# Two attentions on one core: image loads moved behind the copies of f and g, those copies on two queues, and the last reciprocals taken from PSUM

## Chip, cores, metric

The kernel runs on one core of one Trainium2 chip. The metric is the device time of one execution in microseconds (us). Ratios are the mean time of one kernel's runs over that of the other's from the same rounds, so they are not quite the ratio of the medians that I quote beside them.

## The reference, cut to what matters

```python
# x: (8, 64, 64, 64) float32, n = 4096 positions an image
f, g, hh = Wf@x + bf, Wg@x + bg, Wh@x + bh        # 8, 8 and 64 channels
beta = softmax(f^T g, axis=2)                      # 4096 x 4096 an image
x = x + hh @ beta^T                                # layer 0
xn = group_norm(x); q, k, v = split(w_qkv @ xn + b)
x = x + w_proj @ (softmax(q^T k / 8) v)^T + b_proj  # layer 1
```

## The kernel before

An image is two halves of 2048 columns on 64 partitions each. Every layer of every image is four chunks of 512 columns per half; a chunk is 16 steps of scores (TensorE), exponentials (ScalarE), weighted sums (TensorE) and running sums of the exponentials (VectorE). The parts that the change touches:

```python
    def load_x(b):                                  # four loads of 256 KB by SyncE
        ...
                nc.sync.dma_start(t[ts(h, C), ts(k, NH // 2)], x[b, ...])
    load_x(0)                                       # at the very start
    ...
        def project(self, k):                       # f and g of half the columns
            ...
            nc.scalar.activation(full, ps, AF.Identity, bias=fgb)
            nc.vector.tensor_copy(high, full)
            nc.vector.scalar_tensor_tensor(split, high.bitcast(F32), lowmask, full, ...)
            for j in range(2):
                for h in range(2):
                    for p in range(2):
                        for i, (dst, half) in enumerate(((self.f, h), (self.g, p))):
                            nc.sync.dma_start(dst[rows, cols], split[ts(2*j+i, 32), half, :])
    ...
        # finish(): the sums of a chunk, three works for later steps
            def sums(spare):                        # TensorE, ScalarE copy, four small DMAs
            def reciprocals():                      # 128x8, to DRAM, broadcast back to r
            def result():                           # raw * r, then residual and output
    ...
    for b in (1, 2):
        load_x(b)                                   # scheduled early: SyncE is free then
    ...
    # after all chunks: check that every reciprocal lies in range, count the bad ones
    reg = nc.values_load(n_bad[0:1, 0:1], ...)
    with tc.If(reg > 0):
        general_path(tc, *args)                     # a slow path for sums out of range
```

Instructions are placed on each engine's stream by a scheduler at build time, by readiness and then by program order.

## Time and profile before

| | us |
|---|---|
| median of six runs | 3189.54 (3187.82 to 3190.85) |
| span in the trace | 3188.0 |
| first exponential | 22.49 |
| fourth, tenth exponential | 25.22, 35.04 |
| half-clock stretch of TensorE at the start | 20.44 to 30.68 |
| last weighted sum ends | 3169.25 |
| result of the last chunk | 3181.91 |

The page and the timeline are shown in the prediction. In all views SPq, ACTq and PEldq are the sequencers of SyncE, ScalarE and TensorE, which issue copies, wait and branch. Here are lines of the chain of waits at the start (start, length, what), then two groups by source line (durations min/median/max in ns, first and last start):

```profile
16.85 1.50 SPq L381
19.03 2.54 DMA fg_l<-split_l
22.49 2.86 ACT e_l L623 x3
26.20 4.97 PE acc_l L122 x12
```

```profile
L312 DVE RECIPROCAL stash<-zh_l x64: 193/203/205, 98.7 to 3175.1; 128x8 f32<-128x8 f32 x64
L64 PEldq COMPARE_BRANCH  x1: 3595/3595/3595, 3178.6 to 3178.6; - x1
```

The reader sees a start that goes from SyncE's issues to the landing of a copy, to exponentials, to twelve weighted sums at half clock (4.97 us; later dozens take 2.73 in the same chain). The branch on the flag takes TensorE's sequencer 3.6 us (3178.56 to 3182.16), hidden before because the last chunk still waits for its transfer (landed at 3180.34, result at 3181.91). The 128x8 operations of 203 ns in the prediction are the reciprocals of L312.

### The profile page before, as it was taken

The page shows a single profiled execution, that of the slowest core. Times are in us where ns is not written, and L with a number is a line of the kernel's source. Part 1 is how long each engine was busy: PE and PEld are TensorE (multiplying, and loading weights), DVE is VectorE, ACT ScalarE, POOL GpSimd, SP SyncE. Part 2 cuts the span into 40 slices and gives each one's busy share as a digit, 9 for nine tenths or more (in the row PEclk, how much of TensorE's full clock was granted, in tenths as well). Part 3 has the DMA queues.
Part 4 walks back from the last instruction along what each step waited for, and adds up shares of the span by engine and source line. Part 5 has one row for each costly group of instructions (what it writes and reads, how often), then busy time and mean ns, then how long its engine had stood idle before and what let it go on. Part 6 is the DMA issues. An engine that isn't in the chain of part 4 may idle for free.

```text
span 3188.0 us, 58576 instructions
## 1 busy us (share of the span) xinstructions
PE 3116.8 (98%) x25525; PEld 1106.0 (35%) x25525; DVE 2450.2 (77%) x1588; ACT 2083.4 (65%) x2257; POOL 16.7 (1%) x41
## 2 busy tenths in 40 slices
PE   7999999999999999999999999999999999999997
PEld 2333334333333334333333333333333333334432
DVE  6899766887678876788767887679866798666665
ACT  6787655776557765577655875558855587555554
POOL 2000000000000000000000000000000000000000
PEclk9999999999999999999999999999999999999999
DMA  3100010100101001010010100101001000000000
GB/s 69 34 8 17 11 34 8 28 21 8 35 8 28 21 8 34 8 28 21 8 34 8 31 19 7 38 5 35 18 5 41 2 21 18 5 21 15 9 14 15
DMA packets 66408, 63.54 MB, mean 20 GB/s; under 512 B 39408, under 2 KB 39488, under 8 KB 66144
## 3 DMA queue, kind: packets, MB, share of 16 engines
q1 hardware_dynamic: 65024, 59.56, 7.9%
q8 instruction: 202, 3.31, 0.4%
q14 instruction: 62, 0.51, 0.1%
q0 software_dynamic: 800, 0.15, 0.0%
q10 hardware_dynamic: 320, 0.01, 0.0%
HBM read 25.33 MB, written 8.65 MB: 11 GB/s over the span
## 4 chain that ended last, share of the span: by engine, by line
PE 87%; ACT 5%; DVE 4%; issue 2%; DMA 1%; SPq 0%; DVEq 0%; ACTq 0%
PE acc_l L122 51%; PE s_l L122 31%; ACT e_l L623 5%; DVE esum_l L595 3%; PE z_l L122 2%; PE qk_l L122 1%; PE v_l L122 1%; DMA r_l<-recips 0%; PE fg_l L122 0%; SPq L306 0%; DMA zt_l<-zs_l 0%; DVE split_l L371 0%; DVE vt_l L276 0%; DMA recips<-stash 0%; DMA x<-in_x_dram 0%
## 5 line engine op out<-in xcount | busy, mean ns | idle before, releaser
L623 ACT ACTIVATE e_l<-s_l 128x1024 f32<-128x1024 f32 x2048 | 1967.5, 1025 | 1062.0 <-PE s_l L122 1062.0
L595 DVE TENSOR_TENSOR esum_l<-esum_l,e_l 128x2048 f32<-128x2048 f32 x896 | 2050.6, 2289 | 390.1 <-ACT e_l L623 347.3
L122 PE MATMUL acc_l<-e_l,vt_l 64*64 64x512 f32 (+1 forms) x12288 | 1959.5, 595 | 6.7 <-DVE raw_l L524 5.9
L122 PE MATMUL s_l<-kq_l 64*64 64x512 f32 x8192 | 992.2, 589 | 1.5 <-DVE ve_l L443 1.5
L122 PEld LDWEIGHTS acc_l<-e_l,vt_l 64*64 64x64 f32 (+1 forms) x12288 | 594.2, 134 | 1067.2 <-issue 963.9
L122 PEld LDWEIGHTS s_l<-kq_l 64*64 64x64 f32 x8192 | 343.7, 133 | 543.0 <-issue 534.7
L122 PE MATMUL s_l<-fg_l 32*128 32x512 f32 x2048 | 272.0, 472 | 23.6 <-ACT e_l L623 15.5
L122 PEld LDWEIGHTS s_l<-fg_l 32*128 32x128 f32 x2048 | 108.0, 182 | 345.0 <-ACT e_l L623 213.2
L595 DVE TENSOR_TENSOR esum_l<-e_l,e_l 128x2048 f32<-128x2048 f32 x64 | 146.2, 2285 | 78.4 <-ACT e_l L623 78.4
L320 DVE TENSOR_TENSOR raw_l<-raw_l,r_l 128x512 f32<-128x512 f32 x64 | 44.0, 688 | 84.7 <-DMA r_l<-recips 84.7
L310 DVE TENSOR_TENSOR zh_l<-zt_l 128x8 f32<-128x8 f32 x64 | 10.5, 164 | 106.4 <-DMA zt_l<-zs_l 106.4
L122 PE MATMUL z_l<-esum_l,ones 128*32 128x512 f32 x512 | 68.4, 606 | 1.5 <-DVE vt_l L276 1.3
L524 DVE COPY raw_l<-acc_l 128x512 f32<-128x512 f32 x32 | 22.1, 690 | 41.5 <-PE acc_l L122 41.5
L302 ACT COPY zs_l<-z_l 128x512 f32<-128x512 f32 x64 | 38.2, 597 | 5.1 <-PE z_l L122 5.1
L498 ACT ACTIVATE kq_l<-qk_l,qkb 128x512 f32<-128x512 f32 x64 | 40.7, 697 | 0.0
L122 PE MATMUL qk_l<-xn_l,wqk 64*64 64x512 f32 x256 | 34.8, 611 | 0.0
L122 PE MATMUL v_l<-wvp,xn_l 64*64 64x64 f32 x1024 | 22.1, 223 | 8.4 <-ACT e_l L623 8.4
L122 PEld LDWEIGHTS v_l<-wh,x 64*64 64x64 f32 x1024 | 23.0, 136 | 15.9 <-issue 13.6
L122 PE MATMUL fg_l<-x,wfg 64*64 64x512 f32 x128 | 18.8, 652 | 9.7 <-DVE low L164 9.7
L122 PEld LDWEIGHTS v_l<-wvp,xn_l 64*64 64x64 f32 x1024 | 18.4, 134 | 18.6 <-ACT e_l L623 14.9
L525 DVE TENSOR_TENSOR raw_l<-acc_l,raw_l 128x512 f32<-128x512 f32 x32 | 22.1, 692 | 3.3
L528 DVE SCALAR_TENSOR_TENSOR raw_l<-raw_l,pb,x 128x512 f32<-128x512 f32 x32 | 24.0, 751 | 0.9
(81 smaller groups left out, 299.1 us busy)
## 6 DMA issues: line engine op xcount, KB each, us to landing
fg_l<-split_l SPq DMA_DIRECT2D x256, 64.0 KB, 2.0
r_l<-recips SPq DMA_DIRECT2D x128, 128.0 KB, 2.9
x<-in_x_dram SPq DMA_DIRECT2D x32, 256.0 KB, 4.8
kq_l<-kq_l SPq DMA_DIRECT2D x64, 128.0 KB, 2.3
out_dram<-raw_l SPq DMA_DIRECT2D x64, 128.0 KB, 2.3
zt_l<-zs_l SPq DMA_DIRECT2D x256, 2.0 KB, 1.8
recips<-stash SPq DMA_DIRECT2D x64, 4.0 KB, 1.4
wqk<-in_WqkvT_dram POOLq DMA_DIRECT2D x2, 32.0 KB, 5.3
```

Of the source, the lines that this page charges most:

```text
L122: in_order(nc.tensor.matmul(*args, **kwargs))
L302: nc.scalar.copy(zs, z)
L310: nc.vector.tensor_add(zh, zt[:, 0, :], zt[:, 1, :])
L320: nc.vector.tensor_mul(raw, raw, r)
L498: nc.scalar.activation(self.parts[:, h, cols], ps[:, h, :], AF.Identity, bias=k1["qkb"][:, h : h + 1],)
L524: nc.vector.tensor_copy(raw, acc[0])
L525: nc.vector.tensor_add(raw, acc[1], raw)
L528: nc.vector.scalar_tensor_tensor(o, o, k1["pb"], x_tiles[self.b][:, ts(c, CW)], op0=ALU.add, op1=ALU.add)
L595: nc.vector.tensor_add(esum, first if t == 1 else esum, e)
L623: nc.scalar.activation(e[:, p], ps, AF.Exp, scale=at.scale)
```

## The change

The intent: take loads that nobody needs yet out of the way of the start; issue 16 small copies from two engines; and end without three transfers in series.

```diff
+            queues = (nc.sync, nc.scalar) if self.b == 0 else (nc.sync, nc.sync)
...
-                            nc.sync.dma_start(
+                            sent = queues[i].dma_start(
...
-    for b in (1, 2):
-        load_x(b)
+    with tc.issue_after(layers0[0].sent.ins):
+        for b in (1, 2):
+            load_x(b)
...
+            def at_once():                          # the last chunk only
+                z = ps_s.tile([P, 2, CW], F32, tag="s", name=f"z_{n}")[:, 0, :]
+                for p in range(2):
+                    for h in range(2):
+                        matmul(z[ts(h, C), :], ones, esum[:, p, h, :], start=p == 0, stop=p == 1)
+                nc.vector.reciprocal(r, z)
+                result()
+                bounds(r, 1)
...
+    bounds(stash, 0)                                # the other 504 columns, apart
     while later:
         later.pop(0)[2]()
...
+    matmul(bad_ps, bad[:, 0:1], ones[:, 0:1], start=True, stop=False)
+    matmul(bad_ps, bad[:, 1:2], ones[:, 0:1], start=False, stop=True)
```

(`ones` becomes 64 wide, the stash loses eight columns, and `bounds` holds the four operations of the old check.)

More of the change, by code (lines that the diff above doesn't have):

```diff
@@ L62 @@
     fast_path(tc, n_bad, *args)
-    reg = nc.values_load(n_bad[0:1, 0:1], min_val=0, max_val=P)
+    reg = nc.values_load(n_bad[0:1, 0:1], min_val=0, max_val=2 * P)
     with tc.If(reg > 0):
@@ L177, in fast_path @@
     make_identity(nc, ident)
-    ones = const.tile([P, 32], F32, name="ones")
+    ones = const.tile([P, C], F32, name="ones")
     nc.vector.memset(ones, 1.0)
@@ L197, in fast_path @@
     QP = 2 * CW // P
-    stash = const.tile([P, 2 * B * NC * QP], F32, name="stash")
+    stash = const.tile([P, (2 * B * NC - 1) * QP], F32, name="stash")
     recips = [dram.tile([P, QP], F32, name=f"recips_{i}") for i in range(2 * B * NC)]
@@ L297, in sums @@
                         matmul(
-                            z[ts(2 * h + p, 32), :], ones, esum[:, p, h, :],
+                            z[ts(2 * h + p, 32), :], ones[:, 0:32], esum[:, p, h, :],
                             start=True, stop=True, tile_position=(0, 32 * (2 * h + p)),
@@ L317, in reciprocals @@
                     nc.sync.dma_start(r[ts(h, C), :], row.partition_broadcast(C))
+            def at_once():
+                z = ps_s.tile([P, 2, CW], F32, tag="s", name=f"z_{n}")[:, 0, :]
+                for p in range(2):
+                    for h in range(2):
+                        matmul(
+                            z[ts(h, C), :], ones, esum[:, p, h, :], start=p == 0, stop=p == 1
+                        )
+                nc.vector.reciprocal(r, z)
+                result()
+                bounds(r, 1)
             def result():
@@ L321, in result @@
                 self.residual(raw, c)
+            if index == 2 * B * NC - 1:
+                return (at_once,)
             return sums, reciprocals, result
@@ L384, in project @@
                             )
+                            if i == 0:
+                                self.sent = sent
         def scores(self, ps, t, p, c):
@@ L601, in weigh @@
                 delay = NT
-            sums, reciprocals, result = at.finish(acc, esum, c, i)
+            works = at.finish(acc, esum, c, i)
+            if len(works) == 1:
+                at_step(now, works[0])
+                return
+            sums, reciprocals, result = works
             at_step(now + delay, lambda: sums(spare), not spare)
@@ L633, in fast_path, with bounds @@
         weigh(*r, len(seq) * NT)
+    bad = const.tile([P, 2], F32, name="bad")
+    bad_ps = ps_a.tile([P, CW], F32, tag="a", name="bad_ps")[0:1, 0:1]
+    def bounds(recip, i):
+        ok = work.tile(list(recip.shape), F32, tag="zs", name=f"ok_{i}")
+        nc.vector.tensor_scalar(ok, recip, 1.0 / SUM_MAX, None, op0=ALU.is_ge)
+        nc.vector.scalar_tensor_tensor(
+            ok, recip, 1.0 / SUM_MIN, ok, op0=ALU.is_le, op1=ALU.mult
+        )
+        least = small.tile([P, 1], F32, tag="least", name=f"least_{i}")
+        nc.vector.tensor_reduce(least, ok, axis=AX.X, op=ALU.min)
+        nc.vector.tensor_scalar(bad[:, i : i + 1], least, -1.0, 1.0, op0=ALU.mult, op1=ALU.add)
+    bounds(stash, 0)
     while later:
         later.pop(0)[2]()
-    ok = work.tile(list(stash.shape), F32, tag="zs", name="ok")
-    nc.vector.tensor_scalar(ok, stash, 1.0 / SUM_MAX, None, op0=ALU.is_ge)
-    nc.vector.scalar_tensor_tensor(ok, stash, 1.0 / SUM_MIN, ok, op0=ALU.is_le, op1=ALU.mult)
-    least = small.tile([P, 1], F32, tag="least", name="least")
-    nc.vector.tensor_reduce(least, ok, axis=AX.X, op=ALU.min)
-    bad = small.tile([P, 1], F32, tag="bad", name="bad")
-    nc.vector.tensor_scalar(bad, least, -1.0, 1.0, op0=ALU.mult, op1=ALU.add)
-    ps = ps_s.tile([P, 2, CW], F32, tag="s", name="bad_ps")
-    matmul(ps[0:1, 0, 0:1], bad, ones[:, 0:1], start=True, stop=True)
-    nc.vector.tensor_copy(n_bad, ps[0:1, 0, 0:1])
+    matmul(bad_ps, bad[:, 0:1], ones[:, 0:1], start=True, stop=False)
+    matmul(bad_ps, bad[:, 1:2], ones[:, 0:1], start=False, stop=True)
+    nc.vector.tensor_copy(n_bad, bad_ps)
 @with_exitstack
```

## The prediction

> **What bounds the kernel now.** I read the page from the top. It shows one core at full clock and an engine that is hardly ever idle:
>
> ```profile
> span 3188.0 us, 58576 instructions
> PE 3116.8 (98%) x25525; PEld 1106.0 (35%) x25525; DVE 2450.2 (77%) x1588; ACT 2083.4 (65%) x2257; POOL 16.7 (1%) x41
> PE 87%; ACT 5%; DVE 4%; issue 2%; DMA 1%; SPq 0%; DVEq 0%; ACTq 0%
> ```
>
> TensorE is busy 98% of the span and holds 87% of the chain of waits. The steady middle (some 3,100 us of scores and weighted sums) is not touched by the diff: from image 1 on, f and g still go by one queue, and every chunk but the last still sends its sums through DRAM. So all that can move lies in the two ends. I took the timeline and the chain of waits for the first 45 us and from 3165 us on, then the busy times of a few stretches.
>
> The start, from the timeline. First column: start; second: length.
>
> ```profile
> 9.30 0.36 DVE L159 COPY wfg<-w 128x64 f32<-128x64 f32 x1 [8.31 <-DMA x<-in_x_dram]
> 14.95 11.01 SPq L381 DMA_DIRECT2D fg_l<-split_l  x16
> 22.49 5.61 ACT L623 ACTIVATE e_l<-s_l 128x1024 f32<-128x1024 f32 x6 [6.34 <-PE s_l L122]
> 26.12 5.04 PE L122 MATMUL acc_l<-e_l,vt_l 128*64 128x512 f32 x12
> 32.21 10.04 SPq L381 DMA_DIRECT2D fg_l<-split_l  x16
> ...
> 20.50:30.60 10.10, 8.46 (x23) 2.83 (x23) 4.20 (x2) 5.61 (x6) 0.00 (x0) 0.50 0.60 148
> ```
>
> The reader sees that nothing computes before 9.3 us (weights and image 0 have to land among nine image loads), that SyncE then needs 11.01 us to issue 16 small copies (0.63 us each without the one hitch), and that the first exponential waits for the sixth of them until 22.49. The last line (of the stretches' table; the columns are the engines' busy times, then the granted clock) shows TensorE at half clock from 20.5 to 30.6 us, after its idle stretch.
>
> The end, from the timeline and the chain of waits:
>
> ```profile
> 3169.44 1.06 PE L122 MATMUL z_l<-esum_l,ones 128*32 128x512 f32 x8 [0.18 <-PE acc_l L122]
> 3170.56 0.59 ACT L302 COPY zs_l<-z_l 128x512 f32<-128x512 f32 x1 [3.60 <-PE z_l L122]
> 3173.00 1.78 DMA zt_l<-zs_l
> 3175.34 1.39 DMA recips<-stash
> 3177.30 3.04 DMA r_l<-recips
> 3180.43 0.69 DVE L320 TENSOR_TENSOR raw_l<-raw_l,r_l 128x512 f32<-128x512 f32 x1 [2.51 <-DMA r_l<-recips]
> 3181.16 0.75 DVE L528 SCALAR_TENSOR_TENSOR raw_l<-raw_l,pb,x 128x512 f32<-128x512 f32 x1
> ```
>
> The last matmul of the weighted sum ends about 3169.3; the result is ready at 3181.91. The 12.6 us between are a serial walk through three transfers. Then 6.1 us follow to the end: output issue (1.15), landing, and the closing waits.
>
> [...] between 0.8 and 3.6 us SyncE and ScalarE issue four loads each, eight in 2.8 us, against 0.63 us a copy for SyncE alone. [...] The trace has only 128x8 ones: 203 ns, against 166 ns for an addition of the same shape, so it is dearer per element. [...] the branch on the flag (by its line) held TensorE's sequencer 3595 ns. [...]
>
> **The change part by part.**
>
> (1) Images 1 and 2 wait behind f and g. Nine loads of 256 KB go out before 9.7 us, of which the first matmul needs the first two and the weights. The weights were issued by 3.3 us, yet wfg starts at 9.30, and I read that as small packets waiting among large ones. Image 0 stays in their way, and its own last piece would land near then. Dropping images 1 and 2 there should give 0.7 us (estimate; nothing to 1.7). Image 1 is first needed at step 20, about 65 us, so its later load is hidden.
>
> (2) f on SyncE, g on ScalarE. The copy that released the first exponential was SyncE's sixth, the second of the two h rows: issued at 19.03, landed at 21.56. With four-and-four it is the third on each queue, at 14.95 + 2 x 0.63 = 16.2 instead of 19.03: 2.8 us earlier. But ScalarE's stream then holds 8 issues, 8 x 0.63 = 5.0 us, and the second bias addition (1.11 us) ahead of its first exponential: 14.95 + 5.0 + 1.1 = 21.1 instead of 22.49. So I count 1.4 us, which with (1) makes 2.1. For the second half of f and g, ScalarE issues eight more (5.0 us) in the middle of exponentials. Part hides behind queued ones, but a ScalarE that is busy 2.86 of each 3.39 us (three exponentials to a round of matmuls) has little slack, and in the start TensorE is cold and slower anyway. I charge 0.8 us. Net of (1) and (2): 1.3 us gained.
>
> (3) The last chunk's reciprocals from PSUM. Removed from the path: sums (1.10), copy (0.59), issues up to the last (1.83, 3171.17 to 3173.00) and its landing (1.78), addition and small reciprocal (0.18 + 0.21), store (1.39) and broadcast load (3.55, 3176.79 to 3180.34). From 3169.44 to 3180.43 that is 10.99 us with gaps. Added: four fp32 matmuls of 64 columns, two side by side instead of four: the 128*64 weighted sums run 12 in 2.79 us, 0.23 each, so 8 x 0.23 = 1.9 us. Then a reciprocal of 128x512. From 8 elements I get its slope: an addition is 158 + 1.036 n ns (166 at 8, 688 at 512); with that base the reciprocal costs (203 - 158) / 8 = 5.6 ns an element, 3.0 us at 512; with the base of a one-element operation (about 148), 6.9 ns and 3.7 us. I take 3.4. If the 37 ns are a mere fixed latency, it is 0.7. So 1.9 + 3.4 + 0.1 of gaps = 5.4 instead of 10.99: 5.6 us gained at the result.
>
> (4) The other sums are checked apart. 504 columns need 0.43 + 0.69 + 0.69 + 0.15, some 2.0 us of VectorE, that depend on nothing late; VectorE has 1.14 us idle in each 3.43 us round near the end. I expect them placed there, free. The last chunk's own check (2.1 us of VectorE, then matmul and cast: 3175.34 to 3177.93 before, 2.59 us) used to run in the shade of the r transfer; now it comes after the result. The flag is then loaded and branched on. Before, TensorE needed from the load at 3178.0 to 3182.2 (0.5, then a branch of 3.6), all hidden. Now, from the result: 2.6 + 0.5 + 3.7 + 0.1 = 6.9 us until TensorE is through, plus 1.0 for the last waits, 7.9, against 6.05 before. That gives back 1.8 us.
>
> Sum: 1.3 + 5.6 - 1.8 = 5.1 us; 3190.0 - 5.1 = 3184.9. The start may also spare some of the 10 us of half clock if TensorE's idle stretch shrinks, so I put the centre at 3184.3.
>
> **Rivals.** First, the tail becomes the bound: check, flag and branch replace the broken-up transfers, and the saving at the result is mostly lost. The 3.6 us branch speaks for it; against it, the output's own landing needs 3.8 us after the result in any case. It leaves 3187 or so. Second, ScalarE becomes the bound at the start: if its eight issues stand in one row before exponentials that TensorE awaits, or wait for the second split while exponentials queue behind, up to 5 us come back, and the time is 3188 to 3190. Its 65% busy over the whole run speaks against, its 84% in these rounds for. Third, the reciprocal is as cheap as a copy: then 2.7 us more are gained, 3181.5. Fourth, TensorE never drops to half clock: in the cold stretch 12 matmuls took 5.04 us that take 2.79 warm, so with the scores up to 4 us more, 3180. Fifth, the check of the 504 columns stands just ahead of the reciprocal: 1.5 us lost.
>
> **Range and chances.** A gain of 2% would be 64 us; the two ends that change together hold under 60 us, most of it needed. A loss of 2% would need the middle to be rescheduled for the worse, and its code is the same. The three runs before spread over 2.4 us. Stacking the cheap outcomes gives 3179.5, the dear ones 3188.5.
>
> **What would show it.** In the trace after: f and g issue half as long and the first exponential at 20 to 21 us (right), or still past 22 with ScalarE's queue ahead of it (second rival); the weights' copy at about 8.6; the half-clock stretch present or gone; a RECIPROCAL 128x512 with a mean of 3.0 to 3.7 us, or 0.7; the checks of 504 columns between additions of exponentials, before the last matmul; the result about 5.6 us sooner after the last weighted sum; some 8 us from it to the end. I'd be wrong if the middle changed length by more than 1 us, or if the loads now issued near 30 us held up copies that matmuls wait for.

## More of the kernel before

The variants ran later in three batches, on three chips, where the kernel before had medians of 3190.48 to 3190.77.

The tenth exponential is my mark for "steady": from there to past the first chunk, two traces keep one distance.

## The result

The changed kernel takes 3188.45 us (3188.06 to 3189.98, six runs) against 3189.54; ratio 0.9998, interval 0.9985 to 1.001: the same. The span in the trace fell by 2.1 us, from 3188.0 to 3185.9. Its page:

```profile
span 3185.9 us, 58567 instructions
PE 3120.4 (98%) x25527; PEld 1108.3 (35%) x25527; DVE 2455.2 (77%) x1591; ACT 2082.6 (65%) x2256; POOL 16.8 (1%) x41
PE 85%; DVE 6%; ACT 5%; issue 2%; DMA 1%; SPq 0%; ACTq 0%; DVEq 0%
```

The start of the changed kernel, from the timeline (start, length, engine, what, idle time before and what seemed to end it):

```profile
14.17 15.45 SPq L396 DMA_DIRECT2D fg_l<-split_l  x16
14.17 7.18 ACTq L396 DMA_DIRECT2D fg_l<-split_l  x8
21.46 1.11 ACT L380 ACTIVATE full_l<-fg_l,fgb 128x1024 f32<-128x1024 f32 x1 [9.36 <-DMA fg_l<-split_l]
22.47 2.84 ACT L645 ACTIVATE e_l<-s_l 128x1024 f32<-128x1024 f32 x3
24.65 5.28 ACTq L396 DMA_DIRECT2D fg_l<-split_l  x8
26.09 5.39 PE L122 MATMUL acc_l<-e_l,vt_l 128*64 128x512 f32 x12
29.98 5.61 ACT L645 ACTIVATE e_l<-s_l 128x1024 f32<-128x1024 f32 x6 [4.66 <-DMA fg_l<-split_l]
```

ScalarE issues copies for 7.18 us, then for 5.28 us more between its third and fourth exponential. The profile puts its idle time (9.36 and 4.66 us) down to a DMA that landed. What filled it are the issues on ScalarE's own sequencer in the lines above; issuing is not counted as busy. The first exponential has not moved (22.47 against 22.49), the fourth is 4.76 us later, the tenth, at 36.61, 1.57 us later. The second dozen of weighted sums shows why; in the chain of waits it now hangs on these late exponentials, where before it followed the first dozen on TensorE without a gap:

```profile
29.99 2.86 ACT e_l L645 x3
...
32.89 0.50 PE s_l L122 x2
33.39 2.73 PE acc_l L122 x12
```

It starts 1.57 us later than before (33.39 against 31.82), so the whole delay of the steady rounds is ScalarE's row; TensorE, which sat idle for 0.42 us before 32.89, would have waited at any clock. Two lines of the chain of waits show what stretched the first eight issues, and one of the stretches shows the clock (engines' busy times, then the granted clock):

```profile
16.44 4.38 DMA fg_l<-split_l
...
20.84 0.51 ACTq L396
```

```profile
18.10:31.60 13.50, 10.22 (x25) 3.21 (x25) 2.54 (x3) 5.48 (x6) 0.44 (x1) 0.50 0.52 132
```

The eighth issue waited until the copy that ScalarE had issued at 16.44 landed. In this trace SyncE's and ScalarE's copies take turns on eight completion semaphores (107, 109 to 113, 115 and 117), and the issues of a row, from the second on, each wait on the semaphore that they will signal, which the copy eight before has to signal first. Two issuers come round to the ninth twice as fast: the issues at 19.12, 20.02 and 20.84 each follow such a landing (19.10, 20.00, 20.82) by 0.02 us. Each time it is ScalarE's own copy of four issues before, which took 4.3 to 4.4 us to land. (SyncE's issues at 18.94 and 19.51 follow landings at 18.93 and 19.50 in the same way.) Of the 2.1 us that the eight issues took beyond eight times 0.63, these waits are about 0.8 (0.2 to 0.4 us each), and about 1.0 is one issue that was drawn out to 1.64 us.

The end, from the timeline, and the branch by its source line:

```profile
3171.07 1.94 PE L122 MATMUL z_l<-esum_l,ones 128*64 128x512 f32 x8 [0.19 <-PE acc_l L122]
...
3173.04 3.36 DVE L327 RECIPROCAL r_l<-z_l 128x512 f32<-128x512 f32 x1 [0.64 <-PE z_l L122]
3176.44 0.69 DVE L332 TENSOR_TENSOR raw_l<-raw_l,r_l 128x512 f32<-128x512 f32 x1
...
3177.38 0.75 DVE L545 SCALAR_TENSOR_TENSOR raw_l<-raw_l,pb,x 128x512 f32<-128x512 f32 x1
...
3179.92 0.14 DVE L676 CAST n_bad<-bad_ps 1x1 int32<-1x1 f32 x1 [0.28 <-PE bad_ps L122]
```

```profile
L64 PEldq COMPARE_BRANCH  x1: 3355/3355/3355, 3180.7 to 3180.7; - x1
```

From the end of the last weighted sum to the result now takes 7.24 us instead of 12.66, and from the result to the end of the span 7.79 instead of 6.05; together 15.04 instead of 18.71. So the trace's balance is: 1.57 us lost at the start, 0.06 lost over the whole middle (the last exponential is 1.63 later), 3.67 won at the end, 2.04 net. The 0.06 is a net of swings: by about the 960th exponential the lag had grown to 2.55.

### The profile page after: what moved, and what is told of

Its sections match the earlier page's. It is cut to its first block, busy times and chain, and to the rows that moved or that the text cites. A ratio compares the mean times of both kernels' runs of the same rounds, so it can differ in the third digit from the quotient of the medians.

```text
span 3185.9 us, 58567 instructions
## 1 busy us (share of the span) xinstructions
PE 3120.4 (98%) x25527; PEld 1108.3 (35%) x25527; DVE 2455.2 (77%) x1591; ACT 2082.6 (65%) x2256; POOL 16.8 (1%) x41
## 3 DMA queue, kind: packets, MB, share of 16 engines
q10 hardware_dynamic: 1088, 1.06, 0.1%
## 4 chain that ended last, share of the span: by engine, by line
PE 85%; DVE 6%; ACT 5%; issue 2%; DMA 1%; SPq 0%; ACTq 0%; DVEq 0%
PE acc_l L122 50%; PE s_l L122 31%; ACT e_l L645 4%; DVE esum_l L613 4%; PE z_l L122 2%; PE qk_l L122 1%; PE v_l L122 1%; DMA r_l<-recips 0%; PE fg_l L122 0%; DMA zt_l<-zs_l 0%; SPq L306 0%; DVE split_l L385 0%; DMA recips<-stash 0%; DMA fg_l<-split_l 0%; DVE vt_l L276 0%
## 5 line engine op out<-in xcount | busy, mean ns | idle before, releaser
L122 PE MATMUL z_l<-esum_l,ones 128*32 128x512 f32 (+1 forms) x512 | 69.9, 612 | 1.5 <-DVE vt_l L276 1.3
L380 ACT ACTIVATE full_l<-fg_l,fgb 128x1024 f32<-128x1024 f32 x16 | 17.9, 1120 | 10.3 <-DMA fg_l<-split_l 9.4
```

Of the source, the lines that this page charges most:

```text
L122: in_order(nc.tensor.matmul(*args, **kwargs))
```

## The experiments

Theory A: the start lost its gain to ScalarE's own instruction stream, because copies stand in it in rows. Rival B: the images, now loaded at 29.7 us and later, hold up copies or matmuls. All variants were correct and each ran in five timed rounds. "Shift" is the start of the tenth exponential less 35.04; "clock" is when the first half-clock stretch ends; "end" is from the last weighted sum to the end of the span. All but the first two columns come from one trace each. The lag doesn't stay what it was at the tenth exponential: up to the last one, the variants lost up to 2.0 us against the kernel before (g_pool_half; warm_four alone gained, 0.4), with the same code in the middle. Extra half-clock windows are part of that; the rest is not explained. A span or a median therefore says little about a stage here.

| run | median us | ratio to before | 1st exp. | 4th exp. | shift | clock | end |
|---|---|---|---|---|---|---|---|
| before | 3189.54 | 1 | 22.49 | 25.22 | 0 | 30.68 | 18.71 |
| changed | 3188.45 | 0.9998 | 22.47 | 29.98 | +1.57 | 31.67 | 15.04 |
| tail_only | 3187.76 | 0.9991 | 22.53 | 25.26 | +0.51 | 31.75 | 14.97 |
| defer_one_queue | 3187.08 | 0.9986 | 21.57 | 24.29 | -0.34 | 31.04 | 15.51 |
| half_queue | 3186.99 | 0.9988 | 22.43 | 25.14 | -0.62 | 29.51 | 14.78 |
| four_copies | 3185.09 | 0.9980 | 20.48 | 23.29 | -1.81 | 29.01 | 15.40 |
| spread | 3186.70 | 0.9987 | 22.45 | 25.20 | +0.17 | 31.07 | 15.01 |
| g_pool | 3187.13 | 0.9987 | 20.49 | 23.22 | -1.46 | 29.88 | 14.89 |
| no_last_check | 3187.74 | 0.9991 | 22.27 | 29.78 | +3.06 | see text | 12.48 |
| half_recip | 3183.09 | 0.9977 | 21.01 | 23.74 | -2.32 | 27.52 | 13.20 |
| warm_four | 3180.14 | 0.9971 | 20.84 | 23.57 | -2.49 | 28.14 | 12.29 |
| warm_all | 3186.78 | 0.9990 | 20.26 | 24.72 | +0.27 | none | 12.33 |
| g_pool_half | 3183.64 | 0.9977 | 20.74 | 23.46 | -1.58 | 29.27 | 13.14 |

The intervals of the ratios are 0.0013 to 0.0014 wide on either side, so a single ratio settles little here; the stages in the traces do, with one trace each.

**tail_only**: the new tail, the old start.

```diff
-            queues = (nc.sync, nc.scalar) if self.b == 0 else (nc.sync, nc.sync)
+            queues = (nc.sync, nc.sync)
-    with tc.issue_after(layers0[0].sent.ins):
-        for b in (1, 2): load_x(b)
+    for b in (1, 2): load_x(b)
```

> The new tail with the start of the kernel before (nine image loads first, f and g by SyncE alone). Both theories: first exponential at 22.5 us, seventh at 31.6, no shift of the middle against the kernel before; from the end of the last weighted sum to the end of the span 15.0 us instead of 18.7, so a span near 3184.3, some 1.6 us under the changed kernel.

The end took 14.97 us as expected: the tail's gain is its own. Its span, 3185.4, is 1.1 us above what I expected: 0.51 from the start, 0.69 from the middle. The shift is a surprise that helps: with the start of the kernel before in the source and its first exponentials within 0.04 us, the steady rounds are 0.51 us late. Its half-clock stretch ended 1.07 us later. A dozen of weighted sums took 5.39 us at half clock there, against 2.80 at full clock in the kernel before, so I count work at half clock as half, and 1.07 / 2 is 0.53. So I correct shifts by half the difference of the "clock" column before I compare them (an estimate from this one pair of traces). That holds where the steady rounds wait for TensorE, as they do in the chains of tail_only to g_pool in the table. In the changed kernel they wait for ScalarE, so its 1.57 us are not corrected.

**defer_one_queue**: as above, but with the images still behind f and g.

> New tail, images 1 and 2 behind f and g, but f and g both by SyncE. Theory A (ScalarE's own stream of issues is the loss): the weights' copy at 8.6 instead of 9.3, everything from there to the steady rounds 0.7 us earlier than with the kernel before, first exponential at 21.7, fourth at 24.5, seventh at 30.9, span near 3183.6. Theory B (the images, now loaded late, hold up copies or matmuls): the seventh exponential or a later one is 1 us or more behind the kernel before, span 3185 or more.

The weights' copy began at 8.48 instead of 9.30, the first exponential came 0.92 us sooner, and the steady rounds 0.34 sooner, 0.5 by the correction. Nothing up to there is held up by the late images, and the deferral is worth about what the prediction gave it. The span, 3185.4, was the one that B named, not A's 3183.6. But the time went in the middle (0.96 us) and at the end (15.51), and tail_only, whose images come early, lost 0.69 in the middle too; so B fails, as far as one trace each can tell.

**half_queue**: g by ScalarE in the first half only.

```diff
+            queues = (nc.sync, nc.scalar if self.b == 0 and k == 0 else nc.sync)
```

> The changed kernel, but g goes by ScalarE only in the first half of image 0; its second half by SyncE. Theory A: fourth exponential at about 25.2 right behind the third instead of 29.98; first one still near 22.5, because ScalarE's first eight issues (7.2 us) stay; the steady rounds within 0.3 us of the kernel before, span near 3184.3. Theory B: fourth exponential as here, but the steady rounds stay 1.5 us late, span near 3186.

From the timeline of this run:

```profile
14.33 6.99 ACTq L396 DMA_DIRECT2D fg_l<-split_l  x8
...
22.43 5.59 ACT L645 ACTIVATE e_l<-s_l 128x1024 f32<-128x1024 f32 x6
```

Six exponentials in a row, with no gap behind the third, and a corrected shift of -0.04: A holds. The first eight issues still take 7 us, so the first exponential stays at 22.4. The gain of the deferral is swallowed by them.

**four_copies**: only the four copies of g that the first scores need go by ScalarE.

```diff
+   sent = (nc.scalar if i == 1 and self.b == 0 and k == 0 and j == 0 else nc.sync).dma_start(
```

> The changed kernel, but only the first four copies of g (those that the first scores need) go by ScalarE, all others by SyncE. Theory A: ScalarE is free for the second bias addition at about 18.1, the first exponential at about 20, 2.4 us sooner; the steady rounds 1 to 2.5 us sooner than with the kernel before, less what the half-clock windows take; span 3181.8 to 3183.5. Theory B: first exponential sooner too, but the steady rounds no sooner than with the kernel before.

ScalarE is through with its issues at 17.8, and the first exponential comes 2.0 us sooner. The steady rounds are 1.8 sooner, 1.0 by the correction.

**spread**: all 16 copies of g by ScalarE, but the second eight one behind each exponential from the third on.

```diff
+   if self.b == 0 and k == 1 and i == 1: pending.append(send); continue
...
+   if i == 0 and j >= 2 and pending: pending.pop(0)()     # in the loop, behind each exponential
```

> The changed kernel, still eight copies of g's second half by ScalarE, but one behind each exponential from the third on, not eight in a row. Theory A1 (only the row of eight hurts; one issue of 0.6 us runs in the sequencer while an exponential of 1.0 us runs): fourth exponential at about 25.3, the steady rounds within 0.7 us of the kernel before, like the variant whose second half went by SyncE. Theory A2 (each issue takes its 0.6 us from ScalarE wherever it stands): about 25.9 and every exponential to the eleventh 0.6 us further behind, the steady rounds 1 to 2 us late as in the changed kernel.

ScalarE in the timeline of this run:

```profile
24.63 0.52 ACTq L399 DMA_DIRECT2D fg_l<-split_l  x1
25.20 1.02 ACT L653 ACTIVATE e_l<-s_l 128x1024 f32<-128x1024 f32 x1
25.22 0.82 ACTq L399 DMA_DIRECT2D fg_l<-split_l  x1
26.12 1.02 ACT L653 ACTIVATE e_l<-s_l 128x1024 f32<-128x1024 f32 x1
26.61 0.51 ACTq L399 DMA_DIRECT2D fg_l<-split_l  x1
```

The issue at 25.22 runs inside the exponential of 25.20 to 26.22, and the next exponential follows at its usual pitch of 0.92. The corrected shift is -0.03. A1 holds: eight issues cost nothing one by one, and 1.6 us in a row. ScalarE's load was not the matter; the order of its stream was.

**g_pool**: g of image 0 by GpSimd.

```diff
+            queues = (nc.sync, nc.gpsimd) if self.b == 0 else (nc.sync, nc.sync)
```

> The changed kernel, but g of image 0 goes by GpSimd in both halves and ScalarE issues none. Theory A (the cost is ScalarE's stream, not the second queue): second bias addition at about 14.3, first exponential at 19 to 20.5, fourth right behind the third, steady rounds 1.5 to 3 us sooner than with the kernel before, span 3181 to 3183.5. Rival (copies land no sooner whatever queue issues them): first exponential at 21.5 or later, as with one queue behind deferred images.

From the timeline of this run:

```profile
14.36 1.11 ACT L380 ACTIVATE full_l<-fg_l,fgb 128x1024 f32<-128x1024 f32 x1 [2.16 <-DVE split_l L385]
14.54 4.20 POOL L396 DMA_DIRECT2D fg_l<-split_l  x8 [4.16 <-DVE split_l L385]
```

The second bias addition follows at once and the first exponential comes at 20.49. A second queue does help, off the engine that the path needs. The span, 3183.4, lies just inside what I expected and the steady rounds, 1.46 sooner, just outside; the corrected gain is 1.1 us. In the trace GpSimd's copies signal eight semaphores of their own (99 to 106 in the changed kernel's trace) and none of its first eight issues waits, so this run takes away the row on ScalarE and the waits for landings together; no run parts the two.

**no_last_check**: the changed kernel without the check of the last chunk, a probe that would not fall back on bad sums of that chunk.

```diff
-                bounds(r, 1)
+                nc.vector.memset(bad[:, 1:2], 0.0)
```

> The changed kernel without the check of the last chunk's reciprocals (its flag column is set to 0; for this data the output is the same, for sums out of range it would not fall back, so this is a probe and no version). If the check, the flag's load and the branch set the end: from the last weighted sum to the end of the span 13.2 us (15.0 less 1.8), bounded then by the landing of the output. If the output's landing sets it anyway: 15.0 us, no change.

The end took 12.48 us instead of 15.04, from the result on 5.45 instead of 7.79: the check and the branch behind it set the end, by more than the 1.8 us I gave them, since the flag is now loaded before the result (cast at 3179.31, result at 3180.91). In the changed kernel SyncE's closing waits stand still for 2.29 us until VectorE has come through its branch at 3184.8; here they don't. Its start repeats the changed kernel's (fourth exponential at 29.78) and then meets a second half-clock stretch from 33.4 to 36.8, which makes the shift +3.06. That is why its time is no better.

**half_recip**: four_copies, with the reciprocal halved.

```diff
+   # sums of 256 columns on 32 rows each; pick has a 1 in row 32*(2h+q) for the columns of h
+   nc.vector.reciprocal(r[:, 0:HW], z[:, 0:HW])
+   for q in range(2):
+       matmul(wide[:, ts(q, HW)], pick[:, q, :], r[:, 0:HW], start=True, stop=True)
+   nc.vector.tensor_mul(raw, raw, wide)
```

> The variant with four copies by ScalarE, and the last chunk's sums taken in halves of 256 columns on 32 rows each, so that the reciprocal is 128x256, then spread by two matmuls with a 0/1 matrix; the check then has 256 columns and stands beside those matmuls. From 3.36 us at 512 and 0.203 at 8 elements: reciprocal 1.76 us; sums 1.05, spreading 1.2. From the last weighted sum to the end of the span 12.0 us instead of 15.0 to 15.4; span 3180.5, less or more 1 by the middle. If the branch on the flag still sets the end, 13 us or more.

From its timeline:

```profile
3169.62 1.75 DVE L335 RECIPROCAL r_l<-z_l 128x256 f32<-128x256 f32 x1
...
3171.42 2.08 PE L122 MATMUL wide_l<-r_l,pick 128*128 128x256 f32 x4 [1.98 <-DVE r_l L335]
```

The reciprocal came as worked out. The end took 13.2 us, not 12.0, mostly because the spreading took 2.08 us: TensorE had dropped to half clock at 3171.19 (in warm_four, still at full clock, it took 1.13). The branch did not set this end, though it is over 13 us: SyncE waited for the output's landing until 3179.5, and VectorE was through its branch at 3179.8, before SyncE asked for it. Against four_copies it saves 2.2 us.

**warm_four and warm_all**: theory C, that the half-clock stretch eats half of what the start saves. In the traces the half-clock stretches before the tail last 3.41, 10.24 and 13.65 us, one, three and four times 3.41, and a later one starts a whole number of such steps of 3.413 us after the first has ended, wherever I looked: 28 in the kernel before (30.68 to 126.25) and in the changed one (31.67 to 127.25), 198 in defer_one_queue (31.04 to 706.9), 314 in four_copies (29.01 to 1100.8). I call such a step a window. That a window's clock hangs on what TensorE did in the one before it was my guess. So I put useless matmuls into TensorE's idle time, on top of half_recip.

```diff
+    def keep_busy(n):
+        for _ in range(n): matmul(idle, ident, x_tiles[0][:, 0:CW], start=True, stop=True)
...
+    keep_busy(4)                                     # behind the values of image 0
+                if i == 0 and j < 6: keep_busy(1)    # warm_all only, behind each score
```

> The half-width variant with four useless 128x512 matmuls (0.85 us each at full clock, worked out from 0.43 us for a half) on TensorE between the values and the first scores of image 0, in its idle stretch. Theory C [...]: the half-clock stretch starts later, after 21 us, or is shorter than 10.2 us; the steady rounds 0.5 to 2 us sooner than in the half-width variant (2.3 us before the kernel before). If the stretch comes from the sparse scores after 20 us and not from the idle time, no change or a loss up to 1 us.

> As the run with four useless matmuls, plus one behind each of the first six scores, where TensorE waits for exponentials. Theory C: no half-clock stretch in the first 40 us, the first twelve weighted sums in 2.8 us instead of 5.0 to 5.4, the steady rounds 1.5 to 3 us sooner than in the half-width variant. Rival: the useless matmuls themselves stand in the way (0.85 us each at full clock, 1.7 at half), the steady rounds 1 us or more later than there.

From the timeline of warm_four:

```profile
16.07 3.70 PE L122 MATMUL idle<-x,ident 128*128 128x512 f32 x8
...
24.18 4.49 PE L122 MATMUL acc_l<-e_l,vt_l 128*64 128x512 f32 x12
```

In warm_four the stretch shrank from 10.24 us to 3.41 (24.73 to 28.14) but still lies on most of the first weighted sums: with the idle time filled it came after the sparse scores (TensorE busy 1.98 of the 3.41 us before it). The steady rounds gained only 0.2 us on half_recip, less than the 0.5 expected; how much the phase of the windows gave half_recip (its stretch ended at 27.52, the earliest of all) can't be told from one trace each. In warm_all there was no half clock (granted clock 1.00 from 13 to 32 us, TensorE busy 18.53 of these 19.00), and the twelve weighted sums took 2.79 us, but the fillers stood ahead of scores: exponentials came every 1.48 us instead of 0.91, and the start was lost again. So with the gaps filled the half clock stayed away; that half of what the start saves is lost to it is not shown, and the cure is worth little here.

**g_pool_half**: g_pool with the tail of half_recip.

> The start with g by GpSimd and the tail with the half-width reciprocal. Both gains should add: first exponential at 20.5 us; from the last weighted sum to the end 13.2 us; span 3181 to 3182, within 1 us of the half-width variant with four copies by ScalarE.

First exponential 20.74 and end 13.14, so the parts add; its span of 3182.8 is 0.8 us over what I expected. It met an extra half-clock window in the middle, at 1493.6.

The mean granted clock also goes with the scatter between runs of one kernel: of the 27 executions of the kernel before that were timed beside the variants, the 7 with a granted clock of 0.996 have spans of 3184.8 to 3187.6 us, the 20 with 0.995 or 0.994 of 3187.2 to 3192.8. Here is one stretch of the middle, before and then in defer_one_queue:

```profile
126.30:129.60 3.30, 3.30 (x12) 0.76 (x8) 3.20 (x2) 0.95 (x2) 0.00 (x0) 0.50 0.04 6
```

```profile
126.30:129.60 3.30, 3.30 (x18) 1.02 (x20) 2.91 (x2) 1.56 (x4) 0.00 (x0) 1.00 0.04 2
```

TensorE is busy throughout in both, but at half clock it got through 12 matmuls, at full clock 18; across it defer_one_queue gained 1.6 us, and lost 2.0 in a window of its own at 706.9. Twelve of the thirteen traces have such a window near 126 us, and some a second elsewhere. This stands just before the one near 126 in the kernel before:

```profile
122.84:126.25 3.41, 1.16 (x10) 0.34 (x10) 3.41 (x3) 2.49 (x3) 0.00 (x0) 1.00 0.00 0
```

TensorE, waiting 2.34 us for a copy on VectorE, was busy for 1.16 of these 3.41 us; in the other eleven traces for 1.06 to 1.71. In defer_one_queue the windows, counted on from 31.04 in steps of 3.413 us, lie differently across that wait (busy 2.65 and then 1.83), and the clock stayed at 1.00. Busy time of the window before does not sort all of them, though: the later half-clock windows that I looked at (706.9, 1100.8 in four_copies) each follow one with 2.6 busy.

**The best version** is warm_four: 3180.14 us (3179.41 to 3183.71) against 3190.48 for the kernel before in the same rounds, ratio 0.9971 (0.9958 to 0.9985). The single steps to it are smaller than the scatter; the sum is clear of it, though far from 2%. Little of its lead on half_recip is the useless matmuls' own: of the 2.7 us between the two traces' spans, 0.2 lie in the start, 1.6 in the middle (half_recip had a second half-clock window at 1099.3, warm_four none) and 0.9 at the end, where the spreading met the full clock.

## Why the prediction was right or wrong

The time, 3188.45, fell just inside the upper edge of the range. The predicted gain of 5.7 us against the first three runs came to 1.1 on the medians and 2.0 in the trace, so as a forecast of the change it was wrong. Within 2% was right.

- **Step (1), right in itself.** The weights' copy moved from 9.30 to 8.56 (0.74 us; said 0.7), though tail_only, with the old start, has it at 9.75, so single traces scatter by nearly half a microsecond here. The last of the four 2 KB loads of weights landed 6.48 us after its issue before, 5.44 after; that small packets wait among large ones was my reading of it. In the changed kernel nobody downstream saw it.
- **Step (2), the failed one: "So I count 1.4 us, which with (1) makes 2.1".** The first exponential moved by 0.02 us. I had taken ScalarE's eight issues at 0.63 us each, 5.0 us; they took 7.18, because one issue was drawn out to 1.6 us (about 1.0 us; one of 1.5 was drawn out before, too), and because two issuers share the eight semaphores and the later issues wait for landings (about 0.8). That ate the gains of (1) and (2). With four issues on ScalarE, or none, the first exponential came 2.0 us sooner.
- **Step (2), the second eight: "I charge 0.8 us".** A row delayed the fourth exponential by 4.76 us. Of that, 1.57 us reached the steady rounds; the rest was hidden behind the first weighted sums at half clock, which TensorE was doing anyway. The charge was of the right kind and half of what came. Of the eight issues one ran wholly inside an exponential (24.65 to 25.17, in that of 24.28 to 25.31); the others ended in the gap behind it, the last at 29.93. The second rival named this row, and the 3188 to 3190 us that it led to.
- **The start's balance.** The 2.1 us that did not come and the 0.8 that the row cost beyond its charge are the 2.9 us between the predicted gain of 1.3 and the loss of 1.57. The half-clock stretch ended 0.99 us later than before, but TensorE was waiting for ScalarE then (the chain above), so it adds nothing.
- **Step (3), right.** 5.4 us gained at the result, said 5.6; sums 1.94 (said 1.9), reciprocal 3.36 (said 3.4). With 203 ns at 128x8 and 1.75 us at 128x256 (half_recip) that makes 6.3 ns an element and 0.15 us besides, an estimate from these three. The third rival, a cheap reciprocal, is refuted.
- **Step (4), right.** The 504 columns were checked at 3139 to 3141, far from the path. From the result to the end took 7.79 us, said 7.9; the flag came after 1.94 us and not 2.6, as one of the last check's operations ran between the result's two and the next began before the result ended, while VectorE came through its branch later (3184.8) than TensorE (3184.1). The first rival (the tail gives back) holds as a term, 1.7 us of the 5.4.
- **The fourth rival** (no drop to half clock) did not occur in the changed kernel: its stretch was longer, 13.65 us (18.02 to 31.67) instead of 10.24. It shrank to 3.41 in warm_four and stayed away in warm_all, where useless matmuls filled idle time. So the 0.6 us that the centre added for a shorter one did not come either.

Left open: what drew single issues out to 1.5 us at about 16.5 us in both traces (a 16 KB packet on the DMA queue of kind "instruction" runs then in both, 16.71 to 17.97 before and 16.56 to 17.71 after; whether it is the cause was not tested), why the copies issued around it took about 4 us to land, and how much of a start's gain would remain at a fixed phase of the clock windows.

## What to carry to other kernels

A DMA issued by a computing engine is an instruction in its stream: count it there, ask what stands behind it, and put one behind each long operation rather than eight in a row (here a row of eight left ScalarE idle for 4.66 us and the steady rounds 1.57 us late; one by one, in spread, eight cost 0.0 us after correction). When two queues are to halve an issue time, ask how many transfers may be in flight before the next issue has to wait for a landing (here eight for the two queues: ScalarE's fifth to eighth copies take the semaphores of its first four, and three of them waited 0.2 to 0.4 us each). When a path at the end is shortened, look at once for what used to run in its shade; here the flag and its branch came into the light and took back a third (1.7 of 5.4 us). And before two traces are compared stage by stage, look where the half-clock windows of each lie (in tail_only an end 1.07 us later went with steady rounds 0.51 us late).
